# Both ends of a 32-group graph kernel on one core: load order, product order and buffers changed for the first group, order of the pieces changed for the last two

## The chip, the cores and the metric

One core of one Trainium2 chip. The time is the device time of one execution in microseconds (us). Each kernel was run several times; medians and ranges are given. All runs below were in the fast state. Those from the first repeat on are recorded on two chips (chip 7 for the four experiments that take one part back, chip 14 for the rest); for the first result no chip is recorded. The *profiled span* is the length of one profiled execution, from its first to its last instruction; it is about 1.8 us shorter than the time of that same execution. A program on one core has no other cores to compare with, so the state of a run is read from its time and from the granted clock of TensorE.

Engines: PE is TensorE (PEld its weight load), DVE is VectorE, ACT is ScalarE, POOL is GpSimd, SP is SyncE, which issues the DMAs here; SPq is SP's queue. PE runs "slow" or "cold" below where its matmuls take about twice their usual time, and "warm" otherwise: in the kernel before, the eight matmuls at 47.13 us took 3.78 us, with a granted clock of 0.50 from there to 50.70, where such eight usually take 1.89.

## The reference

128 graphs of 128 nodes with 512 features, one adjacency matrix for all, two layers, each with a residual and a layer norm.

```python
def layer0(x, adj, Wq, Wk, Wv):
    q, k, v = x @ Wq.T, x @ Wk.T, x @ Wv.T
    rel = adj.T * (q @ k.T)                       # per graph, 128 x 128
    rel = rel / norm(rel, axis=2)
    return rel @ v

def layer1(x, adj, Wq, bq, Wk, bk, Wv, bv):       # 8 heads of 64
    scores = q @ k.T / 8 + where(adj == 0, -1e9, 0)
    return softmax(scores) @ v

x = layernorm(x + layer0(x, ...))                 # called x1 below
x = layernorm(x + layer1(x, ...))
```

(Written shorter than the original; shapes and operations are the same.)

## The kernel before

The graphs go in 32 groups of 4, so that a group is a 512 by 512 matrix. Layer 0's query and key weights are multiplied once, at the start, into one matrix M. A group then has five dense products, called m (with M), v0, q, k and v1. Each is done in Strassen's way: seven block products instead of eight, a block product being eight matmul instructions (called simply a product below), with sums of weights made once (`weight_sums`) and sums of tokens made per group. Every product is a `step`; a table says at which slot of a round each product and each small piece (scores, softmax, transposes, stores) is issued, and each engine works in that order.

The start: whole weights loaded, M made column block by column block, masks made by DVE as soon as the adjacency is there.

```python
wq_s = big("yT", "wq0_s")
nc.sync.dma_start(wq_s, chunked(wq0))
wk_s = big("v0", "wk0_s")
nc.sync.dma_start(wk_s, chunked(wk0))
# ... [cut: staged x of group 0, then Wv, adjacency, plain x, layer 1's weights]
nc.vector.tensor_scalar(maskp, adj_sb, 0.0, NEG, op0=ALU.is_equal, op1=ALU.mult)
for a in range(H // 2):
    nc.vector.tensor_scalar(mask.rearrange(...)[:, :, a, :], adj_sb.rearrange(...), 0.0, NEG, ...)
# ... [cut]
for dc in range(C):
    p = ps_a.tile([P, D], F32, tag="a", name=f"pM_{dc}")
    for ec in range(C):
        nc.tensor.matmul(p, wq_p[:, ec, dc]..., quadrants(wk_s[:, ec]),
                         start=(ec == 0), stop=(ec == C - 1))
```

The last group: its x1 was spilled to DRAM and is loaded again for the residual; each graph's output is made in one piece.

```python
def last_residual(g):
    LT["x"] = one.tile([P, G, D], F32, tag="qT", name=f"xr_{g}")
    for h in range(2):
        xr = LT["x"][:, 2 * h:2 * h + 2, :]
        nc.sync.dma_start(xr, X1D[g, h].rearrange("b n d -> n b d"))
        nc.gpsimd.tensor_tensor(xr, xr, bv_b[:, None, :].to_broadcast([P, 2, D]), op=ALU.add)
# ... [cut] in last_out:
    nc.vector.tensor_tensor(o.rearrange("p (h e) -> p h e", h=H), p, rs[...].to_broadcast(...), op=ALU.mult)
    nc.vector.tensor_tensor(o, o, xr, op=ALU.add)
```

The order of the pieces, for the last group but one (`g == NG - 2`) and the last:

```python
s = 32 + 3 * b if g == NG - 2 else (32, 39, 46, 52)[b]
# scores at s, maximum at s + 1, exponentials s + 2 .. s + 5, spills s + 4 and s + 6, reload s + 8
for k, f in zip((11, 12, 13, 15, 16, 19, 22, 23) if g == NG - 2 else (...), pieces):
    at(g, s + k, f, g, b)      # transpose, output, back, rows, sum, statistics, norm, write
```

## Time and profile before

| | before |
|---|---|
| time, first three runs | 2548.76 us (2547.06 to 2553.64) |
| the profiled execution: time, span | 2554.97, 2553.2 us |
| mean granted clock | 0.993 |
| PE busy | 2509.8 us, 98% of the span |
| PE idle before the second group's first product (at 74.97 us) | 22.3 us |
| PE idle in the last 89.57 us | 18.0 us |

A share of 98% says that only 2% of PE's time is idle, and the table says that nearly all of it lies at the two ends. So the middle can be left alone: read the waits of the first 75 and the last 90 us, and nothing else. The lines are in the prediction. Note already here that the profiled execution, at 2554.97, was longer than each of the three timed runs; it will matter.

Two points of the trace serve as landmarks below, because the same instructions stand there in all versions: the first attention scores of the first group (PE, `ps`), and the first attention scores of the last group but one. What lies before the first is "head", after the second "tail".

### The profile page before, as it was taken

The page shows a single profiled execution, that of the slowest core. Times are in us where ns is not written, and L with a number is a line of the kernel's source. Part 1 is how long each engine was busy: PE and PEld are TensorE (multiplying, and loading weights), DVE is VectorE, ACT ScalarE, POOL GpSimd, SP SyncE. Part 2 cuts the span into 40 slices and gives each one's busy share as a digit, 9 for nine tenths or more (in the row PEclk, how much of TensorE's full clock was granted, in tenths as well). Part 3 has the DMA queues.
Part 4 walks back from the last instruction along what each step waited for, and adds up shares of the span by engine and source line. Part 5 has one row for each costly group of instructions (what it writes and reads, how often), then busy time and mean ns, then how long its engine had stood idle before and what let it go on. Part 6 is the DMA issues. An engine that isn't in the chain of part 4 may idle for free.

```text
span 2553.2 us, 41473 instructions
## 1 busy us (share of the span) xinstructions
PE 2509.8 (98%) x14656; PEld 2113.5 (83%) x14656; DVE 1573.1 (62%) x2589; ACT 1015.3 (40%) x3203; POOL 837.1 (33%) x1197
## 2 busy tenths in 40 slices
PE   7899999999999999999999999999999999999997
PEld 5688888888888888888888888888888888888886
DVE  4456666566666556666566666666666566665566
ACT  1233444334434444434444434434443444444452
POOL 4113333233333323332333332333332333333323
PEclk9999999999999999999999999999999999999998
DMA  7254565665666564665655665655655656665553
GB/s 153 66 137 146 164 182 156 162 170 146 176 166 165 162 169 145 183 166 154 176 152 157 179 165 159 176 143 163 182 154 164 170 146 176 165 165 161 157 160 117
DMA packets 509009, 405.79 MB, mean 159 GB/s; under 512 B 37504, under 2 KB 424704, under 8 KB 508800
## 3 DMA queue, kind: packets, MB, share of 16 engines
q1 hardware_dynamic: 508800, 403.13, 57.0%
q8 instruction: 115, 1.88, 0.3%
q14 instruction: 94, 0.77, 0.1%
HBM read 238.36 MB, written 164.63 MB: 158 GB/s over the span
## 4 chain that ended last, share of the span: by engine, by line
PE 97%; DVE 2%; DMA 1%; SPq 0%; issue 0%; ACT 0%; POOL 0%; POOLq 0%; DVEq 0%; ACTq 0%
PE pa_v L274 17%; PE pa_q L274 9%; PE pb_v L274 9%; PE pa_k L274 9%; PE pa_m L274 8%; PE ps L389 5%; PE po L441 5%; PE pst L326 5%; PE pd_v L274 5%; PE po L371 4%; PE pb_q L274 4%; PE pb_k L274 4%; PE pb_m L274 4%; PE pd_m L274 2%; PE pd_q L274 2%; PE pd_k L274 2%
## 5 line engine op out<-in xcount | busy, mean ns | idle before, releaser
L409 ACT ACTIVATE w<-w,nmax 128x128 f32<-128x128 f32 x992 | 385.7, 393 | 435.6 <-DVE nmax L402 367.8
L274 PE MATMUL pa_v<-wc_v,tx 128*128 128x256 f32 x1536 | 363.4, 379 | 0.0
L274 PEld LDWEIGHTS pa_v<-wc_v,tx 128*128 128x128 f32 x1536 | 289.0, 190 | 38.4 <-issue 0.4
L444 DVE STREAM_TRANSPOSE oT<-po 128x512 f32<-128x512 f32 x124 | 88.6, 715 | 335.2 <-PE po L441 335.1
L351 POOL TENSOR_SCALAR ve<-st 128x1 f32<-128x1 f32 (+1 forms) x160 | 37.3, 233 | 681.7 <-DVE st L347 679.1
L469 POOL TENSOR_TENSOR xr<-xr,bv_b 128x512 f32<-128x512 f32 x124 | 157.4, 1270 | 264.8 <-DMA xr<-x1d 234.5
L328 POOL TENSOR_TENSOR sq<-rel 128x128 f32<-128x128 f32 x128 | 51.0, 399 | 431.2 <-DVE rel L327 428.9
L392 DVE SCALAR_TENSOR_TENSOR w<-ps,mask 128x1024 f32<-128x1024 f32 x124 | 150.4, 1213 | 63.0 <-PE ps L389 62.9
L409 ACT ACTIVATION_READ_ACCUMULATOR w<-w,nmax 128x1 f32 x992 | 189.0, 190 | 0.0
L274 PE MATMUL pa_q<-tx,wc_q 128*128 128x256 f32 x768 | 185.0, 384 | 0.0
L274 PE MATMUL pa_m<-tx,wc_m 128*128 128x256 f32 x768 | 182.7, 381 | 2.1 <-ACT s_m L282 2.1
L470 POOL TENSOR_TENSOR o<-o,xr 128x512 f32<-128x512 f32 x124 | 157.6, 1271 | 78.5 <-DVE o L467 68.5
L274 PE MATMUL pa_k<-tx,wc_k 128*128 128x256 f32 x768 | 181.4, 379 | 0.0
L467 DVE TENSOR_TENSOR o<-o,rs 128x512 f32<-128x512 f32 x124 | 86.1, 695 | 152.5 <-DMA o<-od 152.5
L274 PEld LDWEIGHTS pa_q<-tx,wc_q 128*128 128x128 f32 x768 | 143.1, 190 | 37.4 <-issue 14.0
L274 PEld LDWEIGHTS pa_m<-tx,wc_m 128*128 128x128 f32 x768 | 146.8, 191 | 22.7 <-ACT s_m L282 2.5
L285 ACT ACTIVATE s_q<-pa_q,bq_sb 128x256 f32<-128x256 f32 x128 | 53.6, 470 | 275.5 <-PE pa_q L274 275.5
L274 PEld LDWEIGHTS pa_k<-tx,wc_k 128*128 128x128 f32 x768 | 145.9, 190 | 19.8
L366 ACT ACTIVATE x<-x,sh,rstd 128x512 f32<-128x512 f32 x128 | 93.9, 803 | 161.6 <-POOL sh L361 151.1
L402 DVE TENSOR_REDUCE nmax<-w 128x4 f32<-128x512 f32 x248 | 156.3, 671 | 0.1
L428 DVE STREAM_TRANSPOSE wT<-wl 128x1024 f32<-128x1024 f32 x124 | 153.0, 1234 | 0.0
L441 PEld LDWEIGHTS po<-wT,v 128*64 128x64 f32 x1984 | 106.5, 137 | 45.6 <-issue 45.2
(157 smaller groups left out, 5099.9 us busy)
## 6 DMA issues: line engine op xcount, KB each, us to landing
wd<-w SPq DMA_DIRECT2D x248, 256.0 KB, 3.2
wl<-wd SPq DMA_DIRECT2D x496, 128.0 KB, 2.9
xl_x<-in_x_dram SPq DMA_DIRECT2D x256, 128.0 KB, 6.2
x<-in_x_dram SPq DMA_DIRECT2D x64, 512.0 KB, 5.7
x1d<-x SPq DMA_DIRECT2D x64, 512.0 KB, 3.5
xl_h<-x1d SPq DMA_DIRECT2D x256, 128.0 KB, 2.9
od<-oT SPq DMA_DIRECT2D x496, 64.0 KB, 1.8
o<-od SPq DMA_DIRECT2D x124, 256.0 KB, 2.9
```

The lines of the kernel that those rows point to most:

```text
L274: nc.tensor.matmul(bank[:, m, :], l[:, k, m * P:(m + 1) * P], r[:, k, :], start=start and m == 0 and k == 0, stop=(m == 1 and k == 1), ski ...
L326: nc.tensor.matmul(p, XT[g][:, dc, b, :], YT[g][:, dc, b, :], start=(dc == 0), stop=(dc == C - 1))
L366: nc.scalar.activation(h, h, AF.Identity, bias=sh[:, b:b + 1], scale=rstd[:, b:b + 1])
L371: nc.tensor.matmul(p, REL[g][0][:, b, :], V0[g][:, b, :], start=True, stop=True)
L389: nc.tensor.matmul(p[:, s, :, a, :], QT[g][r, a, b, :], KT[g][r, a, b, :], start=True, stop=True)
L392: nc.vector.scalar_tensor_tensor(w.rearrange("p s q a r -> p s (q a r)"), p.rearrange("p s q a r -> p s (q a r)"), HD ** -0.5, mask[:, Non ...
L402: nc.vector.tensor_reduce(nmax[:, s * (H // 2):(s + 1) * (H // 2)], w[:, s].rearrange("p q a r -> p a q r"), axis=AX.XY, op=ALU.max, negat ...
L409: nc.scalar.activation(w[:, s, :, a, :], w[:, s, :, a, :], AF.Exp, bias=nmax[:, i:i + 1], accum_out=sums[:, i:i + 1])
L428: nc.vector.transpose(wT, SOFT[g, b][0].rearrange("p a i r -> p i a r"))
L441: nc.tensor.matmul(p[s * HD:(s + 1) * HD, a, :], V1[g][:, b, h * HD:(h + 1) * HD], wT[:, s * (H // 2) + a].rearrange("p q t -> p (q t)"), ...
L469: nc.gpsimd.tensor_tensor(xr, xr, bv_b, op=ALU.add)
L470: nc.gpsimd.tensor_tensor(o, o, xr.rearrange("p (a f r) -> p f a r", a=H // 2, f=A), op=ALU.add)
```

## The change

The intent is to take PE's waits out of both ends. The number of matmuls stays the same (14656 in both).

- Head. M is accumulated in four PSUM banks as four row chunks of Wq and Wk arrive. v0 comes before m in the first group, with Wv loaded ahead of x; the masks are made later (four of the five mask instructions now copy the first one's result, at about the old cost: 4.19 us for the four instead of 3.87). x's transposed buffers of the first group are other ones, so the second group's can be filled early, and the first group's outputs stand between products of the second group's m.
- Tail. The last group's x1 stays on the chip and gets its bias there, with no reload. The pieces of the last two groups have their own tables of slots. The last outputs are made in halves, and DVE gives work to ACT and POOL.

The core of the diff (cut):

```diff
-    nc.sync.dma_start(wq_s, chunked(wq0))
     wk_s = big("v0", "wk0_s")
-    nc.sync.dma_start(wk_s, chunked(wk0))
+    for ec in range(C):
+        for t, w in ((wq_s, wq0), (wk_s, wk0)):
+            nc.sync.dma_start(t[:, ec], w[ec * P:(ec + 1) * P])
...
+        for ec in range(C):
+            for dc in range(C):
+                nc.tensor.matmul(p[dc], wq_p[:, ec, dc]..., quadrants(wk_s[:, ec]), ...)
...
-            XT[g] = one.tile([P, C, G, P], F32, tag="xT", name=f"xT_{g}")
+            XT[g] = one.tile([P, C, G, P], F32, tag="xT" if g else "x1T", name=f"xT_{g}")
...
     def last_residual(g):
-        LT["x"] = one.tile([P, G, D], F32, tag="qT", name=f"xr_{g}")
         for h in range(2):
-            xr = LT["x"][:, 2 * h:2 * h + 2, :]
-            nc.sync.dma_start(xr, X1D[g, h].rearrange("b n d -> n b d"))
-            nc.gpsimd.tensor_tensor(xr, xr, bv_b[...], op=ALU.add)
+            nc.gpsimd.tensor_tensor(X[g, h], X[g, h], bv_b[...], op=ALU.add)
...
+        if b == G - 1:
+            nc.vector.tensor_tensor(oh, oh, xr.rearrange(...)[:, :, s, :], op=ALU.add)
+        elif s:
+            nc.gpsimd.tensor_tensor(o, o, xr, op=ALU.add)
...
+    QUICK = (
+        (32, (34, 34, 34, 35), (36, 38), 38, (43, 44, 45, 47, 51, 51, 55.5, 56.5)),
+        ...                                  # one row per graph of the last group but one
+    LAST = (
+        (17, (19, 20), (24, 24), (25.5, 27), 31, 33, 33),
+        ...                                  # one row per graph of the last group
...
         todo = [("m", r + 1), ("v0", r + 1)] if r < NG - 1 else []
+        if r < 0:
+            todo.reverse()
...
+    at(-1, 8, masks)
+    at(-1, 41, layer1_weights, "k", "k")
```

## The prediction

> **What bounds the kernel now.** I read the page's shares first, then the busy time of the engines by stretch, then what TensorE (PE) waited for, then the timeline and the chain at both ends. By stretch (columns: length, then busy us and instructions of PE, PEld, DVE, ACT, POOL, then granted clock, DMA share, GB/s):
>
> ```profile
> PE 2509.8 (98%) x14656; PEld 2113.5 (83%) x14656; DVE 1573.1 (62%) x2589; ACT 1015.3 (40%) x3203; POOL 837.1 (33%) x1197
> ...
> 0.00:74.97 74.97, 52.66 (x192) 35.26 (x193) 35.20 (x53) 8.59 (x15) 29.20 (x34) 0.93 0.61 131
> 74.97:151.41 76.44, 73.37 (x360) 62.25 (x361) 34.28 (x57) 23.15 (x53) 14.86 (x19) 1.00 0.28 87
> 1000.00:1077.25 77.25, 77.25 (x457) 65.34 (x457) 48.58 (x80) 31.74 (x101) 25.11 (x37) 1.00 0.58 161
> 2463.63:2553.20 89.57, 71.59 (x450) 60.74 (x448) 58.58 (x92) 37.48 (x150) 31.81 (x46) 0.86 0.40 127
> ```
>
> In the middle PE is busy all of 77.25 us of a group's round; PE is the bound there and nothing but fewer matmuls could shorten it. Only the two ends have idle PE: 22.3 us before the second group begins, 18 us in the last stretch. The waits of PE, over the whole run (total us, times, longest), name them:
>
> ```profile
> PE pM L165 <- DMA wk_s<-in_L_gnn_Wk_dram: 10.1, 1, 10.1
> PE pb_v L274 <- DVE yT L289: 7.2, 1, 7.2
> PE po L534 <- DVE wT L526: 6.7, 4, 2.3
> PE po L441 <- DVE wT L428: 4.4, 1, 4.4
> PE pa_m L274 <- DVE xT L189: 2.1, 1, 2.1
> PE pa_m L274 <- ACT s_m L282: 2.1, 1, 2.1
> PE pb_m L274 <- DVE tx L198: 1.0, 1, 1.0
> PE pn L337 <- POOL sq L328: 0.9, 1, 0.9
> ```
>
> All eleven waits of that answer add up to 36.1 us. They also cost speed afterwards, which the timeline shows (start, length, engine, line, operation):
>
> ```profile
> 10.10 16.64 PE L165 MATMUL pM<-wk_s,wq_p 128*128 128x512 f32 x32 [10.10 <-DMA wk_s<-in_L_gnn_Wk_dram]
> ...
> 47.13 3.78 PE L274 MATMUL pb_v<-wc_v,tx 128*128 128x256 f32 x8 [7.24 <-DVE yT L289]
> 50.70 3.04 PE L274 MATMUL pa_m<-tx,wc_m 128*128 128x256 f32 x8
> 53.58 1.89 PE L274 MATMUL pa_v<-wc_v,tx 128*128 128x256 f32 x8
> ```
>
> Eight matmuls that start 1.73 us apart when the engine is warm took 3.6 and 2.9 after the 7.24 us pause: 3 us lost beside the pause itself. The chain of waits at the very end is DVE, POOL and the last store:
>
> ```profile
> 2543.13 3.27 PE po L534 x14
> 2546.42 0.70 DVE o L539
> 2547.15 0.70 DVE o L541
> 2547.87 0.70 DVE bs L346
> 2548.60 0.19 DVE st L347
> ```
>
> From there to 2553.2: reciprocal square root on POOL, 0.55 us of normalizing, 2.9 us of store; 6.8 us behind the last matmul.
>
> **What the Trainium skill says.** "TensorE: Matmul & The Clock Gate", Part 1 (The HAM clock gate): the array idles at half clock and needs about 3.4 us of sustained work to be released. The trace agrees in kind: M's 32 instructions took 16.64 us where the warm 0.43 us each (two of L371 take 0.86) would make 13.8, so 2.9 us lost. [...]Here the DMA rate reaches 2 MB moved at about 8.6 us and Wk is seen at 9.96, so some 1.3 us of it after the data. "SBUF — State Buffer", Who interferes with whom: a DVE instruction with two SBUF inputs blocks against a POOL instruction that reads SBUF. The trace agrees: the weight sums on DVE (128x512) took 1.6 to 1.7 us while POOL worked, 0.69 for the same shape alone.
>
> **The change, part by part: head.**
> (a) M in row chunks. Wq and Wk come as four pairs of 512 KB, and the four products accumulate in four PSUM banks, chunk outermost, so PE can begin on pair one. From the rate of before (0.72 MB moved at 4.5 us, then 0.3 to 0.37 MB/us) I put the first pair's landing at 5.2 us and, with a copy of 0.4 us, PE's start at 5.8 instead of 10.1. Later pairs come every 1.65 us, less than a cold chunk takes (8 x 0.86), so PE isn't starved. M ends at 5.8 + 13.8 + 2.9 = 22.5 instead of 26.75: gain 4.2.
> (b) v before m, Wv ahead of x. Before, m came first and DVE had its additions behind mask making and v's weights (DVE worked without a break from 23.3 to 47.7 us), which is the 7.24 us wait. Now v's weights are transposed and summed first: Wv lands at about 15 us (3 MB at 0.2 MB/us after 8.6, plus 1.3), four transposes of 0.65 and four sums of 0.7 end at 20.6; x's last half lands at 20.3; its transposes follow to 24.6. v's first product finds its operands at 22.5. Its six products (6 x 1.73), two of m, the last of v and five more of m run to about 47.7, with one wait of 1 us before m's last product (it follows its seventh directly, and DVE must have read the bank). m's sums of weights end on DVE by 31, m starts at 32.9. The masks' 4.5 us lie beside m. Then the scores: 0.9 us wait for ACT, 3.6 of matmuls, 0.9 for the squares, 0.4 the norm: 53 us. Masks, mask copies and layer 1's weights move, but cost PE nothing.
> (c) First group's outputs. Before, its four output products and layer norm held the second group's m back, with 2.1 + 1.0 + 2.1 + 0.7 + 0.5 us of waits. xT has another buffer now and is transposed right after the norm, so m of the second group starts at 53 + 1.3 = 54.3, and the four output products (3.44) stand between its first products. The third product of that m: before at 82.03, now at 54.3 + 2 x 1.73 + 3.44 + 0.3 = 61.5. From there both run the same products. Head gain: **20.5 us**, (a) included.
> Layer 0's outputs come back as x1T when q begins, 29.5 us after 54.3, at 84. DVE ends with them near 64 to 65, POOL 2, ACT 2.9, spill 3, reload of the second half to about 78: it fits with 6 us.
>
> **Tail.** From the point where the last but one group's first scores start (2457.52) the products to the last projection add up to 58.2 us warm, to 2515.8; before they end at 2523.5, for the 4.39 us wait, the slow 1.97, 2.54 and 1.49 after it and an idle us. The cause there: DVE stands in order behind a reload (4.46 us) and the spill of the fourth graph left only at 2493.26, as the SP queue was busy. Now scores of three graphs come earlier, DVE transposes before it multiplies the reloaded rows, the last group's residual needs no reload (2 DMAs of 512 KB less), and the fourth graph's product stands later. I followed each queue: spill 2490.5, reload landed 2500, transpose 2501.3, PE asks at 2505. So no wait: dense end near 2516, gain 7.5.
> Then 32 transposes (0.55 per four: 4.4) and four graphs' outputs (8.1 warm): 12.5 of work, 22.9 before (2523.5 to 2546.4). Halved outputs, four transposes in a row and ACT and POOL for a copy, additions and normalizing take DVE out of it; my walk gives 13.2, so the last matmul at 2529.3. But DVE then has 29.7 us of work from 2501.3 on, so it ends at 2531 at best, with the last half's add, statistics, POOL and normalizing at 2534.6, store to 2537.5; with POOL's adds blocking it now and then I take 2539.5. Tail gain: **13.7 us**.
>
> Middle: the order differs only in the two spills of x1 standing together; PE has no wait in it, so zero.
> Sum: 20.5 + 13.7 = 34.2; 2548.8 - 34.2 = **2515 us**.
>
> **Rivals.** (1) The tail becomes DVE's: 58.58 of its 89.57 us are busy already, and 14 us fewer would make it 77%. If three or four of its waits lie badly, the gain falls to 7 or 8: 2521. For: in-order queue, more instructions. Against: adds and copies leave it. (2) Data late at the head: Wv and x now stand behind the chunks, with 512-byte pieces at 0.2 MB/us; 2 or 3 us late starve v, and a pause makes the array slow again: 2519. Against: x has about 1 us, v's sums 2 us to spare. (3) POOL's late k weights (8 us) block DVE's sums in the second group's round: 2 to 4 us more, 2518. Against: DVE is under half busy there. (4) Everything hides: bare PE work is 2536.3 (first to last matmul) - 26 of waits - 13.7 of cold running = 2496.6; with 5.8 before, 2.9 cold and 5.5 behind the span is 2511 of 2553.2, or 2506 in the median. No schedule of these matmuls does better.
>
> **Range and chances.** The floor is 2506, and rivals 1 to 3 together make 2527: range 2508 to 2523. Faster by over 2% would be under 2497.8, below the floor: 0.02. Slower needs a stall in every round (over 1.6 us in each of 31): 0.01.
>
> **What would show it.** First matmul at 5.8 and v's first product near 22.5; no wait over 1.5 us on PE up to the second group's m at 54; rounds of 77.25 in the middle; no wait of an output product for wT in the tail; last matmul 6 to 9 us before the end. Wrong: a first matmul at 8 or later, x1T late (PE idle near 84), rounds over 77.5, or DVE busy without a break in the last 35 us with PE waiting for it.

## The result, and the profile after

| | before | after |
|---|---|---|
| time of the runs taken together | 2549.53 us (2547.06 to 2553.64, 4 runs) | 2521.31 us (2520.24 to 2521.95, 4 runs) |
| ratio | | 0.9887, 95% interval 0.987 to 0.9904 |
| profiled span | 2553.2 us | 2520.1 us |
| head, to the first scores | 139.9 us | 120.5 us |
| between the landmarks | 2317.6 us | 2317.6 us |
| tail, to the end | 95.7 us | 82.0 us |

A ratio is the mean time of one kernel's fast runs over that of the other's fast runs of the same rounds, so it isn't quite the ratio of the medians quoted beside it. The output is correct. The time fell by 1.1%, which is "the same" at the limit of 2%, and inside the predicted range of 2508 to 2523.

The profile of the changed kernel, shares and stretches (columns as in the prediction: start and end, length, then busy us and instructions of PE, PEld, DVE, ACT and POOL, then granted clock, DMA share, GB/s):

```profile
PE 2498.5 (99%) x14656; PEld 2105.4 (84%) x14656; DVE 1559.6 (62%) x2587; ACT 1020.4 (40%) x3211; POOL 840.5 (33%) x1206
```

```profile
0.00:74.97 74.97, 65.22 (x265) 48.01 (x266) 36.45 (x59) 15.65 (x28) 31.57 (x40) 0.98 0.68 151
...
2300.00:2377.25 77.25, 77.25 (x458) 65.33 (x457) 48.10 (x81) 31.66 (x100) 25.63 (x37) 1.00 0.61 166
2430.20:2520.10 89.90, 78.06 (x537) 65.83 (x535) 65.30 (x106) 45.08 (x165) 39.80 (x61) 0.96 0.50 147
```

In the first 74.97 us PE now works 65.22 us instead of 52.66, and in the last 90 some 78.06 instead of 71.59. A middle round is as before: 77.25 us, all of them busy. The granted clock of that last stretch rose from 0.86 to 0.96. Cut at the landmarks, where the matmuls are the same, PE's busy time fell too: in the tail from 77.77 to 70.17 us, in the head from 114.48 to 110.75. So of the 13.7 us by which the tail got shorter, 7.6 are a shorter busy time of the same 490 matmuls and 6.1 idle time that went; of the head's 19.4, 3.7 and 15.6.

What PE waited for, with total us, times and longest wait:

```profile
PE pM L178 <- DMA wk_s<-in_L_gnn_Wk_dram: 4.3, 1, 4.3
PE pa_v L283 <- DVE xT L197: 2.3, 1, 2.3
PE po L548 <- DVE o L553: 1.4, 2, 1.1
PE pa_m L283 <- DVE xT L197: 1.2, 1, 1.2
PE pn L346 <- POOL sq L337: 0.9, 1, 0.9
```

The waits named before of 7.2 (for m's sums), 6.7 (for the copies of the last group) and 4.4 us (for the transposed weights of the softmax) are gone; the first one fell from 10.1 to 4.3. All ten waits of that answer add up to 13.1 us, the eleven of before to 36.5 (the prediction has 36.1).

The start and the seam between the first and the second group, as the timeline of PE has them (start, length, engine, line, operation, and in brackets the idle time ahead and what ended it):

```profile
4.32 15.43 PE L178 MATMUL pM<-wk_s,wq_p 128*128 128x512 f32 x32 [4.32 <-DMA wk_s<-in_L_gnn_Wk_dram]
22.09 1.97 PE L283 MATMUL pa_v<-wc_v,xT 128*128 128x256 f32 x8 [2.35 <-DVE xT L197]
...
54.11 2.85 PE L283 MATMUL pa_m<-xT,wc_m 128*128 128x256 f32 x8 [1.20 <-DVE xT L197]
56.75 2.73 PE L380 MATMUL po<-v,rel 128*128 128x512 f32 x4
```

M starts 5.8 us sooner. v's first product waits 2.35 us: M ended earlier than x's transposes. The last two lines are a leftover of the old trouble: eight products in 2.85 us and four in 2.73 are slow (1.89 and 1.88 for the same a moment later), and the granted clock of the stretch from 54.11 to 56.75 us was 0.68.

The end of the chain of waits:

```profile
2514.24 0.57 POOL rstd L362
...
2515.46 0.22 POOL ve L360
...
2516.37 0.55 DVE o L571
```

The last matmul began at 2510.57 and ended at 2511.67; DVE's part of the fourth graph is done at 2515.0. Then POOL, which works in order, still has the third graph's small operations to finish (2513.69 to 2515.37) before it may begin the fourth's at 2515.46. This costs about half a us. Normalizing and the store follow. The end came 8.4 us behind the last matmul.

### The profile page after: what moved, and what is told of

Same layout as the page of the kernel before. It is cut to its first block, busy times and chain, and to the rows that moved or that the text cites. A ratio compares the mean times of both kernels' runs of the same rounds, so it can differ in the third digit from the quotient of the medians.

```text
span 2520.1 us, 41502 instructions
## 1 busy us (share of the span) xinstructions
PE 2498.5 (99%) x14656; PEld 2105.4 (84%) x14656; DVE 1559.6 (62%) x2587; ACT 1020.4 (40%) x3211; POOL 840.5 (33%) x1206
## 3 DMA queue, kind: packets, MB, share of 16 engines
q8 instruction: 115, 1.88, 0.3%
## 4 chain that ended last, share of the span: by engine, by line
PE 98%; DVE 1%; DMA 1%; issue 0%; POOL 0%; SPq 0%; POOLq 0%; ACT 0%; DVEq 0%
PE pa_v L283 17%; PE pa_q L283 9%; PE pa_m L283 9%; PE pa_k L283 9%; PE pb_v L283 9%; PE ps L398 5%; PE po L450 5%; PE pst L335 5%; PE po L380 5%; PE pd_v L283 5%; PE pb_q L283 4%; PE pb_k L283 4%; PE pb_m L283 4%; PE pd_m L283 2%; PE pd_k L283 2%; PE pd_q L283 2%
## 5 line engine op out<-in xcount | busy, mean ns | idle before, releaser
L453 DVE STREAM_TRANSPOSE oT<-po 128x512 f32<-128x512 f32 x124 | 88.7, 715 | 331.6 <-PE po L450 331.6
L360 POOL TENSOR_SCALAR ve<-st 128x1 f32<-128x1 f32 (+1 forms) x160 | 36.5, 228 | 628.7 <-DVE st L356 625.7
L398 PE MATMUL ps<-kT,qT 64*128 64x128 f32 x1984 | 144.1, 285 | 0.0
```

The source lines that it names most:

```text
L398: nc.tensor.matmul(p[:, s, :, a, :], QT[g][r, a, b, :], KT[g][r, a, b, :], start=True, stop=True)
```

## The experiments

All were timed in five rounds beside the kernel before, and every output was correct. "Gain" is one minus the ratio, times before's median of those rounds.

### The two kernels again, and each half alone

The question: the two profiled spans differ by 33.1 us, while the first ratio says 28.8. Which is the gain, and do the halves make it up?

The kernel before, unchanged (no diff):

> The kernel before, unchanged. Theory A (the profiled execution of before, 2555.0 us, was one with unusually long cold running of TensorE; what the forecast took from it is 4 to 6 us more than a usual execution gives back): this kernel's times spread over 2546 to 2556, and where its profile lies near 2548 the clock is above 0.993 and the four output products of the last group (3.0 to 3.3 us for 14 matmuls in the profile before) are near 1.8. Rival B (the profile only adds a constant): every profile lies 4 to 6 us above the timed runs, with the same durations as the first profile, clock 0.993.

Measured: 2553.64 us (2551.51 to 2556.99, 14 runs); the same kernel as the reference of these rounds: 2553.26 (2546.52 to 2558.02, 19 runs). Ratio 1.0002 (0.9993 to 1.0012). So the profiled run is not an odd one out (theory A fell), and there is no constant between profiles and times either (rival B fell): the first three runs had fallen low in a wide spread. Whether that was chance, or another chip or hour, can't be told: the first result's chip isn't recorded. All later rounds, on two chips, have medians of 2552.2 to 2553.6 for this kernel.

The changed kernel, unchanged (no diff):

> The changed kernel again, in the same rounds as its two halves. If the halves are independent, its gain is the sum of theirs within 1.5 us, about 28; if they share a stall it is less than the sum by more than 2 us. Its times should spread by under 3 us, as it has hardly any pause of over 1.5 us left.

Measured: 2520.32 us (2519.17 to 2521.76, 4 runs), ratio 0.9872 (0.9856 to 0.9888): a gain of 32.7 us. The changed kernel's 4 runs lie within 3 us, the 33 of the one before within 12.

The head alone, the tail as before:

```diff
 (against the kernel before: all of the change above the line "def last_residual", and)
+        sc, no, ou, de, ln, sp, st, tr = (...)
+    at(-1, 8, masks)
 (last_residual, last_out, last_store and the slots of the last two groups stay)
```

> The changed head (weights in chunks, v first, other buffers, first group's pieces) with the tail of before. From the two profiles the head is worth 19.4 us. Theory A (parts add, and before's usual runs have 0 to 2 us less cold running at the head): 17 to 19.5 us faster than before, about 2531. Rival B (the head's gain is given back later, in the first rounds or in the tail): under 14 us.

Measured: 2535.18 us (2530.75 to 2536.13, 5 runs), ratio 0.9927 (0.9913 to 0.9942): a gain of 18.6 us. In its trace the first scores come at 119.7 us and the tail takes 96.6 us, with the old waits in it (6.6 and 6.7 us for wT).

The tail alone, the head as before:

```diff
 (against the kernel before: x1 kept, halved outputs, QUICK and LAST; loads, M, masks, v0 and m stay)
+        nc.gpsimd.tensor_tensor(X[g, h], X[g, h], bv_b[...], op=ALU.add)
...
-            at(g, 11, last_residual, g)
+            at(g, 2, last_residual, g)
```

> The changed tail (x1 kept on chip, own order for the last two groups, halved outputs) with the head of before. From the two profiles the tail is worth 13.7 us, of which some 4 to 6 is cold running behind the pauses that disappear. Theory A (before's usual runs have warmer tails than the profiled one): 9 to 11 us faster, about 2539. Rival B (a fixed worth): 13 to 14 us faster, about 2535.

Measured: 2537.23 us (2533.78 to 2540.92, 6 runs), ratio 0.9938 (0.9923 to 0.9954): a gain of 15.8 us. Theory A's 9 to 11 us fell; the gain is about that of the profiles. The six runs lie in two clusters, three at 2533.8 to 2534.4 and three at 2540.1 to 2540.9. The profiled one is of the slow cluster, and its timeline has a slow stretch:

```profile
2519.38 1.68 PE L522 MATMUL pwT<-ident,w 128*128 128x128 f32 x8
2520.86 3.52 PE L539 MATMUL po<-v,wT 128*128 128x64 f32 x16
2524.16 1.91 PE L522 MATMUL pwT<-ident,w 128*128 128x128 f32 x8
```

These stand in the changed kernel too, with 1.04, 1.90 and 1.04 us. No wait is ahead of these three; short ones (0.40, 0.81 and 1.06 us) stood in the 9 us before them. Its tail took 84.6 us, 2.6 more than that of the changed kernel. The clusters lie 6 us apart and no fast run of this kernel was profiled, so where the rest comes from is open.

The gains of the halves add up to 34.4 us, against 32.7 together; each has an interval of about 4 us either way, so the two are independent as far as this can tell (the expectation allowed 1.5 us of difference and called 2 a shared stall; 1.7 is neither).

### Why the same kernel spreads by 12 us

Here the repeated profiles answer without a run of their own. The kernel before, first profile, and then the unchanged repeat; the second group's first product, behind the same 2.12 us wait:

```profile
74.97 1.99 PE L274 MATMUL pa_m<-xT,wc_m 128*128 128x256 f32 x8 [2.12 <-DVE xT L189]
```

```profile
73.43 3.35 PE L274 MATMUL pa_m<-xT,wc_m 128*128 128x256 f32 x8 [2.12 <-DVE xT L189]
```

And the changed kernel's repeat, then the experiment with the reload (below), whose head is the changed kernel's:

```profile
52.64 3.54 PE L283 MATMUL pa_m<-xT,wc_m 128*128 128x256 f32 x8 [1.20 <-DVE xT L197]
```

```profile
54.76 1.96 PE L283 MATMUL pa_m<-xT,wc_m 128*128 128x256 f32 x8 [1.20 <-DVE xT L197]
```

The same instructions behind the same waits run at full speed in one execution and at half speed in the next; the granted clock in the two slow stretches that I read, 73.43 to 76.58 of the repeat of before and 54.11 to 56.75 of the changed kernel, was 0.58 and 0.68. The Trainium skill, "TensorE: Matmul & The Clock Gate", Part 1, says that the clock gate judges activity by windows of some 3.4 us that run freely, without regard to the kernel's start. These pairs agree with that, since the same row of short pauses cost speed in one execution and not in another; but no run moves the pauses against the windows, so it stays an inference. Nor is it an even throw: of the nine profiles with the changed kernel's seam (its own two, and six experiments besides the one with the reload), only the one with the reload was warm there; of the four with the old seam, only the first.

Pauses aren't all that varies: the wait for wT was 4.4 us in the first profile of before and 6.3 in the second, and M took 16.64 and 17.04 us. That fewer pauses make a kernel steadier isn't shown. The ranges fall from 11.5 us (before, 33 runs) over 7.1 (new tail only, 6 runs) and 5.4 (new head only, 5) to 2.6 (changed, 4), but a smaller number of runs has a smaller range by itself. And two sets speak against a simple count of pauses: the 14 runs of the unchanged repeat lie within 5.5 us where the 19 of the same kernel in the same rounds take 11.5, and the 19 runs with only the masks moved (below), which keep nearly all the old pauses, lie within 4.5.

### One part of the head taken back

This experiment and the three like it (m first, the reload, the old slots) ran in other rounds, on another chip, than the repeat of the changed kernel that they are compared with; the kernel before had medians of 2552.66 and 2553.26 us there. The differences of the ratios say the same as those of the medians (5.1, 3.6, 6.1 and 5.4 us instead of 5.1, 3.2, 5.8 and 5.2), and no run of these four kernels is as fast as the slowest of the changed kernel's eight.

Whole weights again, the rest of the changed kernel kept:

```diff
-    for ec in range(C):
-        for t, w in ((wq_s, wq0), (wk_s, wk0)):
-            nc.sync.dma_start(t[:, ec], w[ec * P:(ec + 1) * P])
+    nc.sync.dma_start(wq_s, chunked(wq0))
+    nc.sync.dma_start(wk_s, chunked(wk0))
```

> The changed kernel, but Wq and Wk loaded whole, one transfer of 1 MB each (the order of M's products stays by row chunks). Theory (step (a) of the forecast): TensorE starts at 9.7 instead of 4.3 us, M ends near 26.5 instead of 19.8; v's first product, which waits for x until 22.1 in the changed kernel, then starts at 26.5, so the loss is 4.4 us, about 2525. Rival (M's head start is lost anyway, since Wv and x arrive no sooner): loss under 1.5 us. Second rival (the pause before v also costs clock): loss under 3.

Measured: 2525.43 us (2525.12 to 2525.46, 4 runs), ratio 0.9892. That is 5.1 us more than the changed kernel by the medians (2520.32). PE starts at 10.09 instead of 4.32, and v's first product follows M at once:

```profile
25.81 1.89 PE L282 MATMUL pa_v<-wc_v,xT 128*128 128x256 f32 x8
```

In the changed kernel's first profile v's first product came at 22.09 after a wait of 2.35 us for x, so 5.8 us of an earlier start became 3.7 at v and 3.6 at the first scores (124.1 against 120.5). In its repeat that wait was short:

```profile
20.63 1.97 PE L283 MATMUL pa_v<-wc_v,xT 128*128 128x256 f32 x8 [0.39 <-DVE xT L197]
```

Against this one it is 5.2 at v and 5.2 at the first scores (118.9), which is what the times say (5.1). The two differ by when Wv came: DVE began v's transposes at 16.18 us in the first and at 14.71 in the repeat, and x's transposes stand behind them. That is the theory's mechanism, with a size somewhat over that of part (a) of the prediction (4.2).

m before v again:

```diff
-        if r < 0:
-            todo.reverse()
```

> The changed kernel with m before v in the first group, as before; all else (Wv ahead of x, v's weight sums ahead of m's on DVE) stays. Theory: m's second product needs the first weight sum of m, which ends at 26.9 in the changed kernel's profile, and its third the second sum at 28.6: 3 to 4.5 us of waits, 2523.5 to 2525. Rival (the order of the two costs nothing by itself, only the masks and weights behind it did): within 1 us of 2520.5.

Measured: 2523.48 us (2523.02 to 2524.72, 4 runs), ratio 0.9886: 3.2 us more than the changed kernel. The wait is the one expected: m's second product, `pb_m`, stands 2.9 us for DVE's sums of M, which can only be made once M is there; v's sums could be made while M was in work.

The masks alone, on the kernel *before*:

```diff
-    nc.vector.tensor_scalar(maskp, adj_sb, 0.0, NEG, ...)
-    for a in range(H // 2):
-        nc.vector.tensor_scalar(mask..., adj_sb..., 0.0, NEG, ...)
+    def masks():
+        (the same instructions)
...
+    at(-1, 10, masks)
```

> The kernel before with one thing of the change alone: the five mask instructions of DVE (4.45 us) stand behind the first group's three additions of m instead of among v's weight transposes. Theory (step (b) of the forecast: DVE's unbroken run to 47.7 us is what TensorE waits for): the 7.1 us wait of v's second product becomes 2.7 us, and the slow 3 us behind it go too[...]: 4.5 to 7.5 us faster than before, about 2547. Rival (v's weight sums are slowed by GpSimd in any case and fill the gap): the wait stays above 5 us, under 3 us faster.

Measured: 2547.74 us (2544.29 to 2548.82, 19 runs), ratio 0.9983 (0.9976 to 0.999): a gain of 4.3 us (interval 2.6 to 6.1), just under what was expected.

```profile
39.64 1.99 PE L276 MATMUL pb_v<-wc_v,tx 128*128 128x256 f32 x8 [1.06 <-DVE yT L291]
...
64.59 3.43 PE L276 MATMUL pa_m<-xT,wc_m 128*128 128x256 f32 x8 [2.12 <-DVE xT L191]
```

The 7.24 us wait is 1.06 now and the product behind it warm (1.99 instead of 3.78). But a later product was slow in this execution, behind the same 2.12 us wait. By the profiles the gain looks larger: the first scores come at 129.5 us, 8.8 to 10.4 sooner than in the two profiles of before, and the span, 2545.1 us, is 8.1 and 8.4 shorter. Some 3 us of that come from which executions were profiled: those of before were 2 us over its median, this one 0.9 under its own. The other 5 or so lie inside the interval of the timed gain. So one block of instructions moved gives about a quarter of what the head's whole change gives (18.6).

### One part of the tail taken back

The last group's x1 loaded again:

```diff
+        LT["x"] = one.tile([P, G, D], F32, tag="qT", name=f"xr_{g}")
         for h in range(2):
-            nc.gpsimd.tensor_tensor(X[g, h], X[g, h], bv_b[...], op=ALU.add)
+            xr = LT["x"][:, 2 * h:2 * h + 2, :]
+            nc.sync.dma_start(xr, X1D[g, h].rearrange("b n d -> n b d"))
+            nc.gpsimd.tensor_tensor(xr, xr, bv_b[...], op=ALU.add)
...
-            at(g, 2, last_residual, g)
+            at(g, 11, last_residual, g)
```

> The changed kernel, but with the last group's x1 read back from memory (two transfers of 512 KB) as before. Theory: nothing waits for that residual, so the time stays within 1 us of 2520.5. Rival (the reload stands in the same in-order queue as the last spills and reloads of the attention weights, and delays them): 2 to 5 us slower, with a new wait of an output product for wT.

Measured: 2526.14 us (2524.91 to 2527.85, 4 runs), ratio 0.9896: 5.8 us more than the changed kernel by the medians, and a tail of 86.1 us instead of 82.0 in the profile. My theory that nothing waits for the reload fell. The timeline of this kernel, POOL, DVE and PE:

```profile
2474.78 4.68 POOL L508 TENSOR_TENSOR xr<-xr,bv_b 128x1024 f32<-128x1024 f32 x2 [13.42 <-DMA xr<-x1d]
```

```profile
2482.51 0.69 DVE L355 BATCH_NORM_STATS2 bs<-o 128x6 f32<-128x512 f32 x1 [2.51 <-POOL o L479]
```

```profile
2486.57 1.16 PE L515 MATMUL ps<-kT,qT 64*128 64x128 f32 x16 [2.76 <-DVE w L517]
```

Read from the bottom: PE waits 2.76 us for DVE to empty the PSUM bank of the scores, and then two products run slow (1.92 and 2.80 us instead of 1.09 and 1.99). DVE was late since it had stood 2.51 us for POOL's sum of a graph of the group before, an instruction ahead of it in its order. POOL was late since, in its order, it had stood 13.42 us until the reloaded rows came and then had their 4.68 us of bias to add, until 2479.4. SP was late as well: the last reload of softmax rows was issued at 2478.65 instead of 2476.41, after a wait of 2.7 us instead of 0.6 for its spill to land; the two extra loads had been issued 2 us ahead of that spill. The load and the later place of the bias in POOL's order were undone together here, so how much belongs to which is open. PE never waits for the reloaded rows themselves; it waits for what stands behind them in the order of the other engines.

The old slots for the last group but one, the rest of the changed kernel kept:

```diff
-                s, ex, sp, st, pk = QUICK[b]
+                s = 32 + 3 * b
+                ex, sp, st = (s + 2, s + 3, s + 4, s + 5), (s + 4, s + 6), s + 8
+                pk = tuple(s + k for k in (11, 12, 13, 15, 16, 19, 22, 23))
```

> The changed kernel, but the last but one group's attention pieces in the order of before; the last group's new order stays. Theory: the wait of the output product for wT of the third or fourth graph (4.4 and 6.3 us in the two profiles of before) and the cold running behind it (2 us) come back: 5 to 9 us slower, 2526 to 2530. Rival (the last group's own order and its halved pieces carry the tail's gain): under 3 us slower.

Measured: 2525.56 us (2523.68 to 2527.63, 4 runs), ratio 0.9893: 5.2 us more. The tail takes 88.7 us instead of 82.0 in the profile, which is that of the slowest of the four runs. The size is the expected one, the form isn't:

```profile
PE po L548 <- DVE o L553: 2.4, 2, 1.8
PE pwT L531 <- ACT w L524: 1.7, 1, 1.7
PE po L450 <- DVE wT L437: 1.6, 1, 1.6
```

The one wait of 4.4 us for wT came back as 1.6, and in the last group PE waits longer for ACT's exponentials and DVE's outputs. But the idle time of the tail grew by only 2.3 us (14.1 instead of 11.8). The other 4.4 are slow running: PE is busy 74.55 instead of 70.17 us with the same 490 matmuls, as here, where the changed kernel has 1.90:

```profile
2508.23 3.51 PE L548 MATMUL po<-v,wT 128*128 128x64 f32 x16
```

Why ACT and DVE come late there wasn't followed.

### Three more edits on top

From the waits left in the changed kernel came three edits. (a): DVE transposes x before it finishes v's sums of weights. (b): m of the second group, and the first group's outputs, in slots that leave no pause at the seam; layer 1's k weights loaded later. (c): the third graph's residual on DVE, so that POOL is free at the end. All three, then (a) alone and (c) alone:

```diff
 (a)
-        weight_sums(wc["v0"], v21, nc.vector)
+        x_transpose(0, 0, 0)
+        (the first two sums)
+        x_transpose(0, 0, 1); x_transpose(0, 1, 0); x_transpose(0, 1, 1)
+        (the other two sums)
 (b)
+                if kind == "m" and g == 1:
+                    key = {1: -20, 5: -18.5, 6: -13.5, 2: -12, 3: -10}.get(i, key)
 (c)
-        if b == G - 1:
+        if b >= G - 2:
```

> An attempt to beat the changed kernel, three edits: (a) DVE transposes x's first quarter before it sums v's weights, (b) the second group's m begins between the first group's last product of m and its scores, with layer 1's k weights loaded behind the second group's x, (c) the third graph of the last group adds its residual on DVE. The changed kernel's profile has 2.3 us of wait before v, 3.1 us in four waits from 44 to 54, 1.9 us of cold running behind them and 1.4 us of GpSimd at the end: 5.5 to 8 us faster than the changed kernel, 2513 to 2515. Rival (x1's way through memory and back, which had 6 us to spare, becomes the wait): q's first product of the second group's round waits, under 4 us faster.

> Edit (a) alone: the wait of v's first product (2.3 us in the changed kernel's profile, 0.6 to 1.6 in others) goes, or what is left is the landing of x: 1 to 2.3 us faster than the changed kernel, 2518.2 to 2519.5. Rival (x's second half lands last and holds the second product): under 0.7 us.

> Edit (c) alone: GpSimd's 1.27 us addition leaves the last chain, DVE takes two of 0.42 us instead: 0.7 to 1.4 us faster than the changed kernel, about 2519.3. Rival (DVE is the tail's bound, rival 1 of the forecast): 0 to 0.5 us slower.

Measured: all three 2518.92 us (2517.72 to 2520.15, 4 runs), ratio 0.9868; (a) alone 2519.7 (2518.56 to 2520.31, 4), ratio 0.9871; (c) alone 2520.43 (2519.4 to 2522.4, 4), ratio 0.9875. Against the changed kernel's 2520.32 (0.9872) that is 1.4, 0.6 and nothing; all intervals overlap, so only the first may be a gain, and it is far under the 5.5 to 8 us expected of it. Its rival had the size (under 4 us) but not the place: q's first product doesn't wait.

Where the gain of all three went shows in its trace. The first wait after M's start comes only at 70.34, and q's first product stands at 81.41 instead of 85.33 or, in the repeat, 83.74:

```profile
70.34 1.99 PE L294 MATMUL pa_v<-wc_v,tx 128*128 128x256 f32 x8 [1.65 <-ACT s_v L302]
...
2507.53 1.49 PE L559 MATMUL po<-v,wT 128*128 128x64 f32 x8 [1.47 <-DVE o L564]
```

So the head gained 2.3 us on the repeat (first scores 116.6 against 118.9), after paying 1.65 for ACT, which had the first group's layer norm ahead in its order. And (c) moved the wait at the very end: in the trace of (c) alone, too, DVE's added work makes PE's last output wait 1.47 us. POOL is not free sooner for it. Counted from the landmark of the tail, DVE's part of the fourth graph is done at 77.3 us instead of 76.9, POOL's small operations for the third graph at 77.6 instead of 77.3, and POOL's last piece begins at 77.7 instead of 77.4. So taking POOL's addition away bought nothing, as the rival said; whether DVE alone sets the end there isn't separated. I didn't run (b) alone.

## Why the prediction was right or wrong

**What bounds the kernel, and the middle: right.** 2317.6 us between the landmarks in both. All of the gain lies at the ends. Small slips of the forecast's reading: the eleven waits add up to 36.5 us, not 36.1; DVE's run "without a break" from 23.3 to 47.7 us has gaps of 0.47 and 0.44; and the "slow 1.49" of the tail isn't slow, as the changed kernel's scores take 1.49 us at the same place.

**(a), M in chunks: right in kind, each number a little off.** M started at 4.32 instead of 5.8 us and ended at about 19.75 instead of 22.5: it took 15.43 us, 1.6 over the warm 13.8, where I had put 2.9. That difference was luck of the execution and no effect of the chunks: with whole weights M took 15.40 to 17.04 us in five profiles. In this profile the 2.7 us were lost right away, as v's operands weren't ready. Taking (a) back cost 3.6 us at the landmark against this profile, 5.2 against the repeat and 5.1 in time; the forecast said 4.2.

**(b), v first: right.** v's first product was at 22.09 in this profile (forecast 22.5); it is set by x's transposes and not by M. It isn't a fixed time: 20.63 in the repeat, with a wait of 0.39. The wait before m's last product was 0.78 us (1), the norm's products were at 52.49 (53), m's sums of weights were done at 29.8 (31).

**(c), the seam: right up to the clock.** The second group's m started at 54.11 (54.3). Its third product stood at 62.77 instead of 61.5, for the slow stretch of 54.11 to 59.3, which the walk hadn't counted. x1T was in time. Head gain: 19.4 us between the two first profiles (forecast 20.5), 17.8 to 21.0 over the pairings of two profiles each; 18.6 by the timed half. No run takes the seam back alone, so its share of that is argued from the trace.

**Tail: right.** 13.7 us between the first profiles, forecast 13.7; 15.6 against the repeat of before, 15.8 by the timed half. That the first pair fits to a tenth is luck. Inside it, the last matmul ended 73.6 us behind the landmark instead of 71.8, and the end came 8.4 us behind it where the forecast's own numbers give 10.2 (2539.5 - 2529.3) and its list of signs 6 to 9; the two misses cancel. No output product waits for DVE's wT any more (one waits 0.8 us for ACT's copy), and dense work ended at 2497.1. What I called the gain of the order is shared: the reload, named only in passing, costs 5.8 us when put back (4.1 in the profile), the old slots of the last group but one 5.2 (6.7). The last group's own slots and the halved outputs weren't taken back alone.

**The step that was off** is the last: "34.2; 2548.8 - 34.2 = 2515". The 34.2 held: 33.1 by the spans, 32.7 by the repeat. The 2548.8 didn't. It was the median of three runs of a kernel whose runs go from 2546.5 to 2558; in the first repeat its 19 and 14 runs have medians of 2553.3 and 2553.6. With that base the same sum gives 2553.3 - 34.2 = 2519.1, and the repeat measured 2520.3. The profile of before had shown it: I had a profiled execution of 2554.97 in hand, took all my waits from that one, and subtracted them from the median of others.

**Rivals.** The first (the tail becomes DVE's) is partly right: DVE is busy 65.30 of 89.90 us and PE waits for it at 1.1 us at most, but an instruction more there costs what it saves elsewhere, as (c) shows. The second (late data) came as a wait of 2.3 us in one profile and 0.4 in another. The third (late k weights on POOL) shows in no wait of PE. The fourth, the floor of 2506 us, stands: the best version measured 2518.9. (It rests on the low base as well; with the later one it would be some 4.5 us higher.)

**The best version.** All three edits on the changed kernel: 2518.92 us, perhaps 1.4 better than the changed kernel; that lies within the intervals.

## What to carry to other kernels

When a kernel is bound by one engine in its middle, add up that engine's waits at the two ends, and take a walk through the in-order queues of the others: here, what stood *ahead* of the needed instruction in DVE, POOL or the DMA queue decided, more than how long the needed instruction took. Take the gain and the base from the same executions, or repeat the base until its spread is known: here, three runs were 4.5 us off, about what one part of the change is worth. And count the slow running behind pauses beside the pauses themselves: in the tail PE's busy time fell by 7.6 of the 13.7 us.

## What the Trainium skill lacked or had wrong

- "TensorE: Matmul & The Clock Gate", the table of Part 1 and the closing table "Why this matters for your kernels": the clock drops after an idle window of about 3.4 us, and the advice is to leave no idle gap over some 3 us. Here the clock fell behind rows of short pauses, the longest 1.20 us (0.78, 0.23, 0.86 and 1.20 within 10 us: eight matmuls in 2.85 and in 3.54 us instead of 1.89) or 2.12 us (3.35 instead of 1.99), and in other executions of the same instructions it didn't (1.96, in one of nine profiles; 1.99, in one of four). The page does tell of micro-idles that make the clock swing, but gives no number for how short they may be. Smaller matmuls (128x128) stand among these pauses; no run separates the pauses from them.
- "DMA: Bandwidth & Descriptors", Specifications, gives 512 bytes as the least transfer for line rate. The first 20 us of the kernel before, in slices of half a us, show a lower rate with 512-byte pieces in this pattern:

```profile
GB/s 0 0 0 61 135 184 385 410 270 262 254 369 410 332 291 406 386 323 209 202 205 198 216 191 206 212 195 221 190 197 173 178 179 216 194 184 175 179 221 237
```

  Up to slice 18 these are the rows of 2 KB of Wq and Wk (up to 410 GB/s), then come the 512-byte pieces of x and Wv, each DMA into 32 partitions, at about 200 GB/s with the DMA engines as busy. No run separates the size of the pieces from the 32 partitions.
- No page gives a figure for how far the times of one whole kernel spread from run to run in the fast state: here 2546.5 to 2558.0 us for the kernel before (33 runs of the first repeat), 2519.2 to 2522.0 for the changed one (8 runs).
